# Half of the exponentials of some attention steps move from ScalarE to VectorE

## The chip, the core and the metric

The kernel runs on one core of a Trainium2 chip. The metric is the device time of one execution in microseconds (us). Four compute engines matter here: TensorE (PE in the profile; PEld is its loading of weights), VectorE (DVE), ScalarE (ACT) and GpSimd (POOL). Each works through its own instructions strictly in the order in which they were written, and waits for others by semaphores. TensorE writes its results into PSUM; ScalarE and VectorE read them there and write into SBUF.

## What is computed

The reference is a hybrid layer on an image batch of shape (4, 64, 64, 128), so 4 batches of 4096 tokens of 128 channels. All of it is float32.

1. Two 3x3 convolutions and a gate, then a first attention with one head (masked, 4 channels of keys, 16 of values) and a residual.
2. A second attention, over all 4096 tokens of a batch and not masked, with 16 heads of 8 channels:

```python
scores = jnp.einsum('bqhd,bkhd->bhqk', q, k)
probs = jax.nn.softmax(scores.astype(jnp.float32), axis=-1).astype(q.dtype)
attn = jnp.einsum('bhqk,bkhd->bqhd', probs, v).reshape(bsz, seqlen, DIM)
h = x + attn @ wo
ffn = jax.nn.silu(h @ w1) * (h @ w3) @ w2
```

3. Eight experts of 128x128 with the top two of a softmax router, and a residual.

The second attention is by far the largest part: 4 x 16 x 4096 x 4096, about 1.07 thousand million exponentials.

## The kernel before

**Steps.** The second attention is cut into *steps*. A step takes one batch, one group of four heads, one chunk of 512 queries (`c`) and one tile of 128 keys (`kt`); 4096 steps make up the whole. A step has two parts, made by `attention_step` (L774). `scores` lets TensorE multiply keys and queries with four matmuls into two PSUM tiles `s` of 128x1024 (two heads in each), and lets ScalarE turn each into an SBUF tile `e` of exponentials with one ACTIVATE. `values` lets TensorE multiply the exponentials with the values (and with a column of ones, for the sum of the softmax) and add the result up in the one PSUM tile `acc`. `acc` is started anew at the first key tile of a *segment* (most segments are 32 steps long) and copied out by VectorE into `at` at the last (L803 to L808).

**Buffers.** There are three `s` tiles (L134), eight `e` tiles (L130 and L144), one `acc` (L135) and, for all other products of TensorE, one tile `m` (L136). A tile that is asked for again waits until the last readers of its buffer are done.

**Order of the work.** Everything is unrolled in Python, and the class `InOrder` (L95) makes each engine keep the order in which instructions are written. A loop (L1184 to L1209) writes one *turn* after another. A turn does the following:

- `do_step` (L225): write the scores and exponentials of the next step and put it on the list `undone`;
- perhaps `insert` (L241): write one piece of other work, called *filler* here: a piece of a convolution, of the first attention, of a projection, of the feed-forward part or of the experts. A filler is a group of 4 to 16 matmuls into `m` and, often, VectorE instructions that read `m`. `credit` decides whether a turn has one: it grows by `rate` in every turn and is used up by the price that the filler yields (0.46 and 0.6 for the usual ones);
- `finish(2)` (L229): write the values of the oldest steps until only two are undone.

So in a steady stream TensorE's order in the turn of step k is: the scores of step k, a filler or nothing, the values of step k-2. The first attention's steps (`first_step`) pass through the same loop, two `e` tiles each as well. The first 330 us (the first batch's convolutions up to the first keys) and the last 70 us lie outside this stream.

The profile puts almost every instruction on one line, L105, since `InOrder` records them there. So groups are told apart by their tile names: `s<-qx,f_kx` is a score, `e<-s` an exponential, `acc<-e,vg` a value product, `m<-...` filler.

Of the kernel before, what the change touches and what calls it, by code (L numbers as in the profile page):

```python
# [9 lines left out]
FP = mybir.dt.float32  # L10
# [81 lines left out]
    return np.concatenate(list(parts.values()), axis=1), where  # L92


class InOrder:  # L95


    def __init__(self, tc, engine):
        self._tc, self._engine, self._last = tc, engine, None

    def __getattr__(self, name):
        op = getattr(self._engine, name)

        def call(*args, **kw):
            made = op(*args, **kw)  # L105
            if self._last is not None:
                after = mybir.DependencyInfo(mybir.DependencyClass.NoSync, mybir.DependencyReason.DATA)
                self._tc.add_manual_dep(made.ins, self._last, after, reason="as written")
            self._last = made.ins.name
            return made  # L110

        return call
# [3 lines left out]
def fast_path(ctx: ExitStack, tc: tile.TileContext, a: dict, where: dict, out: bass.AP, verdict):  # L116
# [10 lines left out]

    const = ctx.enter_context(tc.tile_pool(name="f_const", bufs=1))
    big = ctx.enter_context(tc.tile_pool(name="f_big", bufs=1))
    ep = ctx.enter_context(tc.tile_pool(name="f_ep", bufs=8))  # L130
    wk = ctx.enter_context(tc.tile_pool(name="f_wk", bufs=2))
    sm = ctx.enter_context(tc.tile_pool(name="f_sm", bufs=2))
    dram = ctx.enter_context(tc.tile_pool(name="f_dram", bufs=2, space=bass.MemoryType.DRAM))
# [15 lines left out]

    def chunk(tag, name=None):  # L150
        return wk.tile([P, QB], FP, tag=tag, bufs=CHUNKS.get(tag, 1), name=name or tag)

    def small(name, dims):
        return sm.tile([P, *dims], FP, tag=name, name=name)
# [64 lines left out]
    seen = const.tile([P, 4, B], FP, name="f_seen")  # L219


    steps_in, undone, fillers, urgent = [], [], [], []
    held, turn = [False], [0]

    def do_step(step):  # L225
        scores, values = step
        undone.append((values, scores()))

    def finish(leave):  # L229
        while len(undone) > leave:  # L230
            values, es = undone.pop(0)
            values(es)

    def advance(part):

# [463 lines left out]
    def first_step(c, r, qx0, sums, found):  # L699

        diagonal = r == c

        if diagonal and c > 0:
            place = [(0, 0, 0), (0, QB, P), (1, 2 * P, 2 * P), (1, QB, 3 * P)]
            spans = [(0, QB + 3 * P), (2 * P, QB + P)]
        else:
            place = [(j // 2, (j % 2) * QB, 0) for j in range(NSLOT)]
            spans = [(0, 2 * QB)] * 2

        def scores():  # L710
            ss, es = [s_tile(), s_tile()], [e_tile(), e_tile()]
            for j, (half, lo, off) in enumerate(place):
                r_ = slice(j * SLOT, j * SLOT + n_row)
                pe.matmul(
                    ss[half][:, lo : lo + QB - off],
                    lhsT=kx0[r_, r, :].bitcast(FR),
                    rhs=qx0[r_, off:].bitcast(FR),
                    start=True,
                    stop=True,
                )  # L720
            for e, s, (lo, hi) in zip(es, ss, spans):
                act.activation(e[:, lo:hi], s[:, lo:hi], AF.Exp)
            parts = []
            for j, (half, lo, off) in enumerate(place):
                e = es[half][:, lo : lo + QB - off]
                if diagonal:
                    at = j * P - off
                    if at:
                        pool.memset(e[:, :at], 0.0)
                    dve.tensor_tensor(e[:, at : at + P], e[:, at : at + P], k_of["tri"], ALU.mult)  # L730
                parts.append((off, e))
            return parts

        def values(parts):
            if r == 0:
                sums.append(acc if alone[0] else m_tile())
            for j, (off, e) in enumerate(parts):
                pe.matmul(
                    sums[0][j * SLOT : (j + 1) * SLOT, off:],
                    lhsT=v0[:, 4 * r + j, :],  # L740
                    rhs=e,
                    start=r == 0,
                    stop=r == c,
                )
            if r == c:
                at = chunk("at0")
                dve.tensor_copy(at, sums[0])
                found.append(at)

        return scores, values  # L750


    def keys(d, g, quarter, place):
# [17 lines left out]
        )  # L771
        return vg

    def attention_step(b, seg, kt, place, qx, vg, part):  # L774
        g, c = seg.g, seg.c

        def scores():
            ss, es = [s_tile(), s_tile()], []
            for j in range(NSLOT):
                r = slice(j * SLOT, (j + 1) * SLOT)  # L780
                pe.matmul(
                    ss[j // 2][:, (j % 2) * QB : (j % 2 + 1) * QB],
                    lhsT=kx[r, place * P : (place + 1) * P].bitcast(FR),
                    rhs=qx[r, :].bitcast(FR),
                    start=True,
                    stop=True,
                )
            for s in ss:
                e = e_tile()
                act.activation(e, s, AF.Exp)  # L790
                es.append(e)
            return es

        def values(es):
            for j in range(NSLOT):
                pe.matmul(
                    acc[j * SLOT : j * SLOT + 1 + HD1, :],
                    lhsT=vg[:, kt // 4, kt % 4, j, :],
                    rhs=es[j // 2][:, (j % 2) * QB : (j % 2 + 1) * QB],
                    start=kt == seg.lo,  # L800
                    stop=kt == seg.hi - 1,
                )
            if kt == seg.hi - 1:  # L803
                at = chunk("at1")
                if part:
                    dve.tensor_tensor(at, acc, part[0], ALU.add)
                else:
                    dve.tensor_copy(at, acc)  # L808
                if seg.hi == NT:
                    urgent.append((turn[0] + 1, lambda: by_token(b, g, c, at)))  # L810
                else:
                    sp.dma_start(out=scratch[b]["p"][g, c], in_=at)

        return scores, values

    def by_token(b, g, c, at):

# [300 lines left out]
    def stream():  # L1118
# [16 lines left out]
        for at, seg in enumerate(plan):  # L1135
            now[0] = seg.b
            while not seg.ready():
                yield None
            late = seg not in ahead
            if late:  # L1140
                bring(seg)
            qx, vg = ahead.pop(seg)
            part = []
            for quarter in range(seg.lo // 8, seg.hi // 8):
                key_quarter(seg, quarter)
            for _ in range(4 if late else 0):
                yield None
            follower = plan[at + 1] if at + 1 < len(plan) else None
            for kt in range(seg.lo, seg.hi):
                steps_left[seg.b] -= 1  # L1150
                if seg.lo > 0 and kt == seg.lo + 4:

                    part.append(chunk("part"))
                    sp.dma_start(out=part[0], in_=scratch[seg.b]["p"][seg.g, seg.c])
                yield attention_step(seg.b, seg, kt, 8 * seg.place(kt // 8) + kt % 8, qx, vg, part)
                if follower and follower not in ahead and follower.ready():
                    bring(follower)
                if kt % 8 == 7:

                    for later in plan[at + 1 :]:  # L1160
                        quarters = [q for q in range(later.lo // 8, later.hi // 8) if later.place(q) == seg.place(kt // 8)]
                        if quarters:
                            if later.ready():
                                key_quarter(later, quarters[0])
                            break
# [17 lines left out]
    credit, waiting = 0.0, False  # L1183
    while True:  # L1184
        turn[0] += 1
        if steps_in:
            do_step(steps_in.pop(0))
        else:
            step = next(steps, False)
            if step is False:  # L1190
                break
            waiting = step is None
            if waiting:
                finish(0)
            else:
                do_step(step)
        b = now[0]
        if batches[b].second == NQ and len(batches) == b + 1 and b + 1 < B:
            Batch(b + 1)
            fillers.append([first_attention(b + 1, batches[b + 1]), PREPARE])  # L1200

        rate = 1.0
        if batches[b].second == NQ:
            within = steps_left[b] - 40 if b + 1 < B else min(steps_left[b] - 40, 160)
            rate = sum(us for _, us in fillers) / max(1, within)
        credit = min(0.7, credit + rate)
        if waiting or credit > 0.0 or urgent and not held[0]:
            credit -= insert()
        finish(2)  # L1209
    finish(0)  # L1210
    while urgent:
        if held[0]:
# [722 lines left out]
```

## Time and profile before

| what | value |
|---|---|
| median of 3 runs | 8379.8 us (8378.74 to 8383.02) |
| profiled execution, its time | 8383.2 us |
| profiled execution, span from first to last instruction | 8381.4 us |
| mean granted TensorE clock | 0.981 |
| ACT busy | 7919.2 us (94%) |
| PE busy | 8082.3 us (96%) |
| DVE busy | 2543.8 us (30%) |
| POOL busy | 711.6 us (8%) |
| exponentials `e<-s` on ACT | 8480, 7836.1 us |
| value products `acc<-e,vg` on PE | 32768, 4362.5 us |
| scores `s<-qx,f_kx` on PE | 16960, 2795.9 us |

A group's row in the profile gives the engine, the operation, the output and inputs, the shape and the count, then after the bar the busy time in us and the mean duration of one in ns, then the idle time of the engine just before the group's instructions and what ended it. Matmuls overlap in time, so that a mean of 598 ns does not say that one takes 598 ns of TensorE; the distance from one start to the next is what counts. A float32 value product appears as two MATMUL records, a score as one; a group of four value products is therefore x8.

### The profile page before, as it was taken

What the parts mean: (1) busy time and instruction counts of PE and PEld (TensorE: products, weight loads), DVE (VectorE), ACT (ScalarE), POOL (GpSimd) and SP (SyncE); (2) the same over time, 40 slices, a digit from 0 to 9 for tenths busy, and PEclk for the clock granted to TensorE, in tenths of its full rate; (3) what the DMA queues carried; (4) which work ended last, traced back from release to release, by engine and by line L of the source; (5) the groups of instructions that cost most, each with busy time, mean ns of one, the idle gap of its engine ahead of it and who ended that gap; (6) DMA issues with size and microseconds to landing.
All of it is one profiled execution on the core that took longest, in us unless ns stands there. A gap on an engine that the chain in (4) does not pass through costs nothing. (4 is left out here: it accounts for less than half of the span.)

```text
span 8381.4 us, 173763 instructions
## 1 busy us (share of the span) xinstructions
PE 8082.3 (96%) x73785; PEld 2565.1 (31%) x73785; DVE 2543.8 (30%) x5279; ACT 7919.2 (94%) x8698; POOL 711.6 (8%) x597
## 2 busy tenths in 40 slices
PE   4899999999999999999999999999999999999998
PEld 3222222223333332333333233233333333332333
DVE  7433122223322223333332222333333332221123
ACT  1899999999999999999999999999999999999996
POOL 5101101000000003110000000311100000000000
PEclk7999999999999999999999999999999999999998
DMA  1221010101100001101110000001101111011110
GB/s 54 76 66 66 19 38 23 40 23 48 44 17 19 22 11 31 33 29 46 34 30 11 26 15 17 28 30 44 33 33 43 37 37 43 31 38 34 54 53 32
DMA packets 239541, 295.99 MB, mean 35 GB/s; under 512 B 81731, under 2 KB 153891, under 8 KB 238755
## 3 DMA queue, kind: packets, MB, share of 16 engines
q1 hardware_dynamic: 234739, 283.03, 10.6%
q8 instruction: 580, 9.50, 0.5%
q10 hardware_dynamic: 4016, 1.77, 0.1%
q14 instruction: 206, 1.69, 0.1%
HBM read 185.12 MB, written 99.61 MB: 34 GB/s over the span
## 5 line engine op out<-in xcount | busy, mean ns | idle before, releaser
L105 ACT ACTIVATE e<-s 128x1024 f32<-128x1024 f32 x8480 | 7836.1, 1083 | 191.0 <-PE s L105 180.7
L105 PE MATMUL acc<-e,vg 128*9 128x512 f32 x32768 | 4362.5, 598 | 61.2 <-DVE at L105 60.4
L105 PE MATMUL s<-qx,f_kx 32*128 32x512 f32 (+1 forms) x16960 | 2795.9, 497 | 68.3 <-ACT e L105 51.4
L105 PEld LDWEIGHTS s<-qx,f_kx 32*128 32x128 f32 (+1 forms) x16960 | 1121.4, 182 | 4074.7 <-ACT e L105 3821.9
L105 PEld LDWEIGHTS acc<-e,vg 128*9 128x9 f32 x32768 | 707.3, 90 | 861.3 <-issue 448.5
L105 PE MATMUL m<-v,f_wino 128*32 128x256 f32 x5360 | 435.1, 397 | 9.6 <-DVE t L105 7.1
L105 DVE TENSOR_TENSOR by_e<-m,gate 128x512 f32<-128x512 f32 x248 | 171.5, 691 | 869.3 <-PE m L105 869.3
L105 POOL TENSOR_TENSOR v<-r 128x1024 f32<-128x1024 f32 x128 | 249.4, 1954 | 1277.4 <-PE m L105 1258.1
L105 DVE COPY sd<-m 128x512 f32<-128x512 f32 x167 | 115.5, 691 | 726.0 <-PE m L105 726.0
L105 PE MATMUL m<-f_we,y2T 128*32 128x256 f32 x3968 | 318.4, 393 | 0.5 <-DVE nt L105 0.5
L105 POOL TENSOR_TENSOR rs<-ve,f_minus_half 128x4 f32<-128x4 f32 x64 | 65.2, 1019 | 2972.5 <-DVE ve L105 2819.6
L105 DVE TENSOR_REDUCE added<-by_e 128x128 f32<-128x1024 f32 x128 | 255.2, 1994 | 4.4
L105 POOL TENSOR_TENSOR t<-t,h 128x512 f32<-128x512 f32 x32 | 40.9, 1278 | 2456.3 <-DVE h L105 2456.3
L105 PE MATMUL m<-hT,f_fw 128*32 128x256 f32 (+1 forms) x2728 | 236.1, 391 | 0.0
L105 DVE TENSOR_TENSOR t<-m,sums 128x256 f32<-128x256 f32 x126 | 53.5, 425 | 465.5 <-PE m L105 465.5
L105 DVE SCALAR_TENSOR_TENSOR h<-m,h 128x512 f32<-128x512 f32 (+1 forms) x93 | 64.2, 690 | 411.3 <-PE m L105 411.3
L105 DVE TENSOR_TENSOR t<-m,t 128x512 f32<-128x512 f32 x62 | 42.9, 692 | 446.3 <-PE m L105 446.3
L105 DVE COPY h<-m 128x512 f32<-128x512 f32 (+1 forms) x93 | 64.2, 690 | 357.0 <-PE m L105 357.0
L105 PEld LDWEIGHTS m<-v,f_wino 128*32 128x32 f32 x5360 | 107.1, 108 | 177.2 <-issue 152.5
L105 DVE COPY at<-acc 128x512 f32<-128x512 f32 x130 | 89.6, 689 | 233.2 <-PE acc L105 232.7
L105 PE MATMUL m<-e,f_v 128*32 128x512 f32 (+2 forms) x1128 | 149.7, 574 | 0.0
L105 DVE TENSOR_TENSOR e<-e,f_consts 128x128 f32<-128x128 f32 x128 | 30.2, 295 | 346.9 <-ACT e L105 346.9
(259 smaller groups left out, 3751.3 us busy)
## 6 DMA issues: line engine op xcount, KB each, us to landing
f_kx<-d_k SPq DMA_DIRECT2D x139, 512.0 KB, 4.1
qx<-d_q SPq DMA_DIRECT2D x152, 256.0 KB, 2.7
d_q<-two SPq DMA_DIRECT2D x64, 512.0 KB, 3.6
vg<-d_v SPq DMA_DIRECT2D x32, 576.0 KB, 4.2
d_k<-two SPq DMA_DIRECT2D x32, 512.0 KB, 3.3
d_v<-vc SPq DMA_DIRECT2D x32, 288.0 KB, 3.1
xe<-in_x_dram SPq DMA_DIRECT2D x32, 256.0 KB, 2.9
xt<-in_x_dram SPq DMA_DIRECT2D x32, 256.0 KB, 3.8
```

The costliest lines, as they stand in the source:

```text
L105: made = op(*args, **kw)
```

## The change

In some steps, called *late* here (a name of the diff), only the first of the two `s` tiles is turned into exponentials by ScalarE. The second is read by VectorE, which computes the exponentials with a scaling, a rounding by adding a large constant, a polynomial of degree five in Horner form, and a shift that makes the power of two. These are 1 instruction of 1024 columns and 16 of 512 columns for each late step. They are not written at once: `settle` writes a few in each turn, as long as an estimate of VectorE's backlog (`dve.load`) is under 1.5 us. When all are written, and three turns have passed, `settle` writes the values of the late step, behind the ordinary values of that turn. At the end of a segment all that is left is written at once. There is at most one late step at a time, and it lies at least 2 steps behind the start of its segment and at least 8 ahead of its end.

The bookkeeping of `credit` follows: a late turn adds 0.92, the turn of the late values takes 0.97. A new tile set (`ea`, `z` of 1024 columns, `t`, `q` of 512 columns, one buffer each) holds the late step, and the pool of `e` tiles goes from eight buffers to five.

```diff
-    ep = ctx.enter_context(tc.tile_pool(name="f_ep", bufs=8))
+    ep = ctx.enter_context(tc.tile_pool(name="f_ep", bufs=5))
...
+    def late_tile(name, n=QB):
+        return ep.tile([P, n], FP, tag=name, bufs=1, name=name)
...
     def do_step(step):
-        scores, values = step
-        undone.append((values, scores()))
+        scores, values, late = step
+        es = scores()
+        if late is None:
+            undone.append((values, es))
+        else:
+
+            slow.append((values, es, late, turn[0]))
...
+    def settle(limit):
+
+        if not slow:
+            return 0.0
+        values, es, todo, since = slow[0]
+        if not todo and (limit is None or turn[0] > since + 2):
+            slow.pop(0)
+            values(es)
+            return 0.97
+        while todo and (limit is None or dve.load < limit):
+            todo.pop(0)()
+        if limit is None:
+            return settle(None)
+        return 0.0
+
+    def powers(z):
+
+        todo = []
+        for h in range(2):
+            zh = z[:, h * QB : (h + 1) * QB]
+            t, q = late_tile("t"), late_tile("q")
+            todo.append(lambda t=t, zh=zh: dve.tensor_scalar(t, zh, MAGIC, None, ALU.add))
+
+            todo.append(
+                lambda t=t, zh=zh: dve.scalar_tensor_tensor(zh, t, MAGIC, zh, ALU.subtract, ALU.subtract)
+            )
+            todo.append(lambda q=q, zh=zh: dve.scalar_tensor_tensor(q, zh, POLY[4], zh, ALU.add, ALU.mult))
+            for k in (3, 2, 1):
+                todo.append(
+                    lambda q=q, zh=zh, k=k: dve.scalar_tensor_tensor(q, q, POLY[k], zh, ALU.add, ALU.mult)
+                )
+            bits = t.bitcast(mybir.dt.int32)
+            todo.append(lambda bits=bits: dve.tensor_scalar(bits, bits, 23, None, ALU.logical_shift_left))
+            todo.append(
+                lambda t=t, q=q, zh=zh: dve.scalar_tensor_tensor(zh, q, POLY[0], t, ALU.add, ALU.mult)
+            )
+        return todo
...
+            if late is not None:
+                e, z = late_tile("ea", 1024), late_tile("z", 1024)
+                act.activation(e, ss[0], AF.Exp)
+                dve.tensor_scalar(z, ss[1], LOG2E, SHIFT, ALU.mult, ALU.add)
+                late.extend(powers(z))
+                return [e, z]
...
         def values(es):
+            if kt == seg.hi - 1:
+                settle(None)
...
-                yield attention_step(seg.b, seg, kt, 8 * seg.place(kt // 8) + kt % 8, qx, vg, part)
+
+                late = [] if not slow and seg.lo + 2 <= kt <= seg.hi - 8 else None
+                yield attention_step(seg.b, seg, kt, 8 * seg.place(kt // 8) + kt % 8, qx, vg, part, late)
...
     while True:
         turn[0] += 1
+        begun, spare = len(slow), 0.0
...
+        if len(slow) > begun:
+            spare = 0.92
+        dve.load = max(0.0, dve.load - 1.84 + spare)
...
-        credit = min(0.7, credit + rate)
+        credit = min(0.7, credit + rate) + spare
...
         finish(2)
+        credit -= settle(1.5)
```

`dve.load` grows in `InOrder` with each VectorE instruction by 0.15 + 0.00106 for each column.

More of the change, by code (lines that the diff above doesn't have):

```diff
@@ L92, in shape_constants @@
     return np.concatenate(list(parts.values()), axis=1), where
+LOG2E = 1.4426950408889634
+SHIFT = 0.4430875400888237
+POLY = (-753.21220293, 522.08671661, -180.9375242, 41.80864673, -7.28773528)
+MAGIC = 12582912.0 + 256 + 117
 class InOrder:
@@ L99, in __init__ @@
         self._tc, self._engine, self._last = tc, engine, None
+        self.load = 0.0
     def __getattr__(self, name):
@@ L105, in call @@
             made = op(*args, **kw)
+            sizes = [int(np.prod(ap.shape[1:])) for ap in (*args, *kw.values()) if hasattr(ap, "shape")]
+            self.load += 0.15 + 1.06e-3 * max(sizes, default=0)
             if self._last is not None:
@@ L219, in fast_path @@
     seen = const.tile([P, 4, B], FP, name="f_seen")
-    steps_in, undone, fillers, urgent = [], [], [], []
+    steps_in, undone, fillers, urgent, slow = [], [], [], [], []
     held, turn = [False], [0]
     def do_step(step):
-        scores, values = step
-        undone.append((values, scores()))
+        scores, values, late = step
[4 more added lines that the diff above has]
+            slow.append((values, es, late, turn[0]))
     def finish(leave):
@@ L748, in values @@
                 found.append(at)
-        return scores, values
+        return scores, values, None
     def keys(d, g, quarter, place):
@@ L772, in values_of, with attention_step @@
         return vg
-    def attention_step(b, seg, kt, place, qx, vg, part):
+    def attention_step(b, seg, kt, place, qx, vg, part, late):
         g, c = seg.g, seg.c
@@ L812, in values @@
                     sp.dma_start(out=scratch[b]["p"][g, c], in_=at)
-        return scores, values
+        return scores, values, late
     def by_token(b, g, c, at):
```

## The prediction

> **What bounds the kernel now.** I read the engine totals first, then the groups of instructions, then the engines by stretch, then the order of time in two single turns. Totals and groups:
>
> ```profile
> PE 8082.3 (96%) x73785; PEld 2565.1 (31%) x73785; DVE 2543.8 (30%) x5279; ACT 7919.2 (94%) x8698; POOL 711.6 (8%) x597
> ...
> L105 ACT ACTIVATE e<-s 128x1024 f32<-128x1024 f32 x8480 | 7836.1, 1083 | 191.0 <-PE s L105 180.7
> ```
>
> ScalarE makes 8480 exponentials and sits idle only 191.0 us ahead of them. TensorE's 96% says less, because its matmuls overlap. By stretch (columns: engine, busy us and count):
>
> ```profile
> 2330.00:3330.00 1000.00, 988.82 (x9034) 304.31 (x9032) 256.15 (x503) 990.55 (x1091) 72.75 (x55) 1.00 0.07 20
> ```
>
> The fourth pair is ACT: 990.55 of 1000 us. In the stream ScalarE is the bound, but with TensorE close behind. One turn with filler, and one without (start us, duration, engine, group):
>
> ```profile
> 4005.65 2.90 ACT L105 ACTIVATE e<-s 128x1024 f32<-128x1024 f32 x3
> 4005.91 0.50 PE L105 MATMUL s<-qx,f_kx 32*128 32x512 f32 x4
> 4006.34 0.64 PE L105 MATMUL m<-v,f_wino 128*32 128x256 f32 x8
> 4006.80 1.04 PE L105 MATMUL acc<-e,vg 128*9 128x512 f32 x8
> ```
>
> ```profile
> 4000.51 0.51 PE L105 MATMUL s<-qx,f_kx 32*128 32x512 f32 x4
> 4000.95 1.05 PE L105 MATMUL acc<-e,vg 128*9 128x512 f32 x8
> 4001.93 0.51 PE L105 MATMUL s<-qx,f_kx 32*128 32x512 f32 x2
> ```
>
> Three exponentials end 2.90 us after the first began and one lasts 1.08, so they start every 0.91 us: 4005.65, 4006.55, 4007.46. A turn has two, 1.81 us. On TensorE a turn without filler takes 1.42 us (4000.51 to 4001.93), one with filler 1.86 (the next scores start at 4007.77). Step k's scores start at 4005.91, its first exponential at 4006.55, its second at 4007.46: 1.55 us after the scores. In the same turn the values of step k-2 start at 4006.80 and end at 4007.84, 1.93 us after the scores. So in a filler turn **the second exponential of step k starts before the values of step k-2 are done**. Without filler the values end at 4002.00, 1.49 us after the scores. Keep these two numbers.
>
> **What the Trainium skill says.** "Perfetto Trace Analysis", section "Identifying Performance Opportunities": the same gap repeating on the engine that should be saturated can mean that there aren't enough buffers for the next tile. Before the change no such gap is seen (191 us in all). Its section "Identifying the Most-Contended Engine" warns that matmul busy time isn't distance to the limit; the trace agrees, since a turn of 1.81 us needs 1.42 without filler. "VectorE: DVE Perf Modes", section "The perf-mode tier table", has fp32 one-source operations within SBUF at twice the rate, and two-source ones or a PSUM operand at the single rate. The trace agrees: the cast `two<-u` takes 441 ns for 512 columns, the two-source `g0T<-th,h` 692, the copy `sd<-m` from PSUM 691.
>
> **The change, part by part.** The instruction order of the changed kernel, built but not run, holds 325 late steps.
>
> *Removed:* 325 exponentials x 0.91 = 296 us of ScalarE, 3.5%.
>
> *Added on VectorE:* per late step one 1024-column read of PSUM (nearest row, `top<-two` of 1024 columns: 1.22 us), 12 two-source instructions x 0.69 = 8.3 and 4 one-source ones x 0.49 (`w<-u`, 486 ns; between 0.44 and 0.64 by the rows) = 2.0: 11.5 us, x325 = 3740 us. VectorE goes from 2544 to about 6280 us, some 70% of its time: not the bound by sum.
>
> *Moved on TensorE:* no matmul is added. The late values come as a second group of 0.97 us in one turn (325 turns, 214 of them with filler too), and the late turn has no values at all.
>
> *The `e` pool, eight buffers to five.* This is where I expect the result to be decided. While step k's exponentials are written, steps k-2 and k-1 still hold two tiles each, as `finish(2)` leaves them; with step k that is six. With five, the second exponential of step k can only start when the first tile of step k-2 is free, that is when the values of step k-2 have been added up. These stand on TensorE behind step k's scores and behind the filler. In the built order the semaphores say so: 3,908 of the 3,915 ordinary second exponentials wait for the value matmuls of their own turn; before, all 4,240 wait for their scores alone.
>
> What the wait costs: the values end 1.93 us after the scores in a filler turn, and ScalarE needs about 0.10 more to see it (at 3083.4 a score ended at 3083.37 and ScalarE started at 3083.47): 2.03 us, against 1.55 before. So 0.48 us late. Without filler 1.49 + 0.10 = 1.59 against 1.55: nearly nothing. What is late next: the first exponential of step k+1, queued behind it, and with it the scores of step k+2, which need that exponential's PSUM tile (1.17 us from the start of a first exponential, 4004.74, to the scores at 4005.91). That closes a loop over two turns: 2.03 + 0.91 + 1.17 = 4.11 us with filler, where ScalarE alone needs 4 x 0.91 = 3.62. A filler turn that follows an undelayed one therefore takes 1.81 + 0.48; one right behind a delayed turn comes free, since the loop spans both. By this rule 1,294 ordinary turns of the built order are delayed (2,560 of 4,237 turns have filler): 1,294 x 0.48 = **621 us**.
>
> Nor does a late step then give its 0.91 back. The turn behind it has scores that wait for the late exponential, then values, then its own second exponential: the same loop, 3.67 us without filler and 4.11 with, for late turn and next. Two ordinary turns without the wait take 3.62. With filler in that next turn (240 of 325): 240 x 0.48 = **115 us**; the others 0. So the 296 us are not gained but swallowed.
>
> *Late values.* They put 0.97 us on TensorE behind the ordinary values, and the next scores wait. Without filler these start at 0.43 + 0.97 + 0.97 = 2.37 us, their exponential 0.60 later at 2.97, where ScalarE would be free at 1.55 + 0.91 = 2.46: 0.51 lost. With filler 3.43 against 2.03 + 0.91 = 2.94: 0.49, or up to 1.0 where an ordinary step follows. I take 0.52: 325 x 0.52 = **169 us**; both ends, 0.25 and 0.8, give 80 and 260.
>
> *Ends of segments.* By the rule of `settle`, 72 polynomial instructions are written at once at segment ends, ahead of the last values: 72 x 0.69 = **50 us**, or 0 if VectorE was ahead.
>
> *VectorE late for others.* `m` has one buffer. A filler's copy may find up to 1.5 + 0.69 us of polynomials ahead; after filler ends at 0.89 us the next `m` product comes at about 2.0 + 0.43, and the copy takes 0.76, so 0.78 is slack. `at<-acc` (154 of them) has less. Unknown: 0 to 150 us; I take **40**. One-source instructions may also meet GpSimd's; that is in the 150.
>
> *Taken back.* Other ACTIVATEs (some 180 in the stream x 0.65) fall half into ScalarE's new gaps: -60. Runs of filler turns that TensorE sets at 1.86 instead of 1.81 now vanish under the wait: about half of them, 1,300 x 0.05 = -65. TensorE's other small stalls: -30. `InOrder`'s count of columns writes no instruction; DMAs are unchanged in number.
>
> Sum: 621 + 115 + 169 + 50 + 40 - 155 = +840 us. On the profiled execution's span of 8381.4 that is 9221; the runs' median lies 1.6 us below that span, so I predict 9220 us.
>
> **Rivals.** (A) *The wait doesn't bind and the relief arrives.* For it: ScalarE is the bound, and 296 us less would show. Then late values still cost 169 and segment ends and lateness 90: 8381 - 296 + 259 = 8344, or 8085 if late values cost nothing and VectorE keeps ahead. It decides once the values end within 1.45 us of the scores in filler turns, where the rows have 1.93. Against it: the five buffers, and the order of TensorE.
> (B) *It binds half as hard*, because filler turns bunch up or the values' first half is done sooner: 368 in place of 736, giving 8840. Against it: the four products of a group run side by side (eight records of 598 ns within 1.04 us), so the first half ends with the second.
> (C) *VectorE becomes the second bound.* If a quarter of some 1,300 refills of `m` find it 0.7 us late beyond the slack, +230: 9440. For it: it is an in-order queue at 70%, and its polynomials stand behind copies that wait for TensorE. Against it: the estimate of the backlog, and longer turns leave it more time.
>
> **How the numbers follow.** Chances: main case 0.75, B 0.10, C 0.10, A 0.05. The main case's own bounds: 0.35 instead of 0.48 takes 200 off, cheap late values 90 more, and dear ones with a late VectorE add 240: about 8930 to 9450. B and C stretch it to 8840 and 9450, which I take as the range. A difference of 0.2% is about what a measurement of this kernel can tell from none. Faster: most of A, 0.04; same 0.01; slower 0.95.
>
> **What would show it.** Right: ACT well below 94% with a large idle time ahead of `e<-s`, ended by PE `acc`, some 0.3 us in many filler turns; 325 exponentials fewer; VectorE near 6200 us; TensorE's groups at the same durations. Wrong: idle time ahead of `e<-s` as small as now, or ended by `s` or by VectorE; or PE waiting for DVE `m` readers for hundreds of us. The prediction fails most easily if the second exponential's wait is released before the values end.

## The result and the profile after

The changed kernel takes 9103.9 us (median of 4 runs, 9095.4 to 9105.2); the kernel before took 8381.4 us in the same session (8378.7 to 8385.3). The ratio is 1.086, with a 95% interval of 1.0841 to 1.0878: slower by 722 us. The profiled execution has a span of 9102.9 us.

Engine totals of the changed kernel, and its group of ordinary exponentials (busy us, mean ns, then idle time ahead of the group and what ended it):

```profile
PE 8489.9 (93%) x73785; PEld 2743.8 (30%) x73785; DVE 6156.8 (68%) x10804; ACT 7823.0 (86%) x8373; POOL 756.0 (8%) x597
...
L116 ACT ACTIVATE e<-s 128x1024 f32<-128x1024 f32 x7830 | 7442.3, 1032 | 953.3 <-PE acc L116 838.5
```

ScalarE has 325 exponentials fewer in all (7830 `e` and 325 `ea` against 8480), as planned. But it is busy 86% instead of 94%, and idle 953.3 us ahead of exponentials instead of 191.0. Nearly all of it, 838.5 us, was ended by `acc`, a value product. In the kernel before no exponential waited for one. The waits of ScalarE (us in total, times, longest) say how often:

```profile
ACT e L116 <- PE acc L116: 838.5, 1498, 14.9
ACT e L116 <- PE s L116: 78.5, 100, 18.6
```

In the order of time one sees where (rows of PE and ACT alone). First the ends of two filler turns of the changed kernel, in a stretch of ordinary steps (start us, duration, engine, group, idle before):

```profile
4061.07 1.04 PE L116 MATMUL acc<-e,vg 128*9 128x512 f32 x8
4062.05 0.51 PE L116 MATMUL s<-qx,f_kx 32*128 32x512 f32 x4
4062.21 3.81 ACT L116 ACTIVATE e<-s 128x1024 f32<-128x1024 f32 x4 [0.21 <-PE acc L116]
...
4065.09 1.04 PE L116 MATMUL acc<-e,vg 128*9 128x512 f32 x8
4066.06 0.51 PE L116 MATMUL s<-qx,f_kx 32*128 32x512 f32 x4
4066.22 4.72 ACT L116 ACTIVATE e<-s 128x1024 f32<-128x1024 f32 x5 [0.20 <-PE acc L116]
```

The values end at 4062.11 and ScalarE restarts at 4062.21, 0.10 later; four exponentials on, two turns later, the same thing happens at 4066.22. Two filler turns take 4.01 us, where the prediction's loop gives 4.11 and two turns without the wait 3.62. Then the surroundings of a late step, whose first tile is `ea`:

```profile
4054.73 1.10 ACT L116 ACTIVATE ea<-s 128x1024 f32<-128x1024 f32 x1
4055.07 0.50 PE L116 MATMUL s<-qx,f_kx 32*128 32x512 f32 x2
4055.67 1.08 ACT L116 ACTIVATE e<-s 128x1024 f32<-128x1024 f32 x1
4055.89 0.49 PE L116 MATMUL s<-qx,f_kx 32*128 32x512 f32 x2 [0.32 <-ACT ea L116]
4056.47 0.66 PE L116 MATMUL m<-f_consts,at 128*128 128x128 f32 x4
4057.06 1.05 PE L116 MATMUL acc<-e,vg 128*9 128x512 f32 x8
4058.03 0.50 PE L116 MATMUL s<-qx,f_kx 32*128 32x512 f32 x4
4058.20 3.80 ACT L116 ACTIVATE e<-s 128x1024 f32<-128x1024 f32 x4 [1.45 <-PE acc L116]
```

ScalarE is done with the late step's one exponential early and then stands for 1.45 us, until the values that end at 4058.11 free its tile. The time that was taken off ScalarE comes back as its idle time. This holds for most late steps: counted in the trace, 295 of the 1,498 waits for values (347.3 of the 838.5 us) stand at just this place, the second exponential behind `ea`.

VectorE's new groups have about the durations that the prediction took for them (0.69 us for instructions with two sources, 0.49 for those with one, 1.22 for the read of PSUM); the column after the bar is busy us and mean ns:

```profile
L116 DVE SCALAR_TENSOR_TENSOR q<-q,z 128x512 f32<-128x512 f32 x1950 | 1408.4, 722 | 54.4
L116 DVE TENSOR_SCALAR z<-s 128x1024 f32<-128x1024 f32 x325 | 397.3, 1223 | 346.9 <-PE s L116 341.5
...
L116 DVE TENSOR_SCALAR t<-z 128x512 f32<-128x512 f32 x650 | 288.3, 444 | 14.5
```

### The profile page after: what moved, and what is told of

The parts are those of the page before. It is cut to its first block, busy times and chain, and to the rows that moved or that the text cites. A ratio compares the mean times of both kernels' runs of the same rounds, so it can differ in the third digit from the quotient of the medians.

```text
span 9102.9 us, 178435 instructions
## 1 busy us (share of the span) xinstructions
PE 8489.9 (93%) x73785; PEld 2743.8 (30%) x73785; DVE 6156.8 (68%) x10804; ACT 7823.0 (86%) x8373; POOL 756.0 (8%) x597
## 5 line engine op out<-in xcount | busy, mean ns | idle before, releaser
L116 ACT ACTIVATE e<-s 128x1024 f32<-128x1024 f32 x7830 | 7442.3, 1032 | 953.3 <-PE acc L116 838.5
L116 PE MATMUL s<-qx,f_kx 32*128 32x512 f32 (+1 forms) x16960 | 3142.2, 498 | 335.8 <-ACT e L116 179.3
L116 DVE SCALAR_TENSOR_TENSOR q<-q,z 128x512 f32<-128x512 f32 x1950 | 1408.4, 722 | 54.4
L116 DVE TENSOR_SCALAR z<-s 128x1024 f32<-128x1024 f32 x325 | 397.3, 1223 | 346.9 <-PE s L116 341.5
L116 DVE SCALAR_TENSOR_TENSOR z<-q,t 128x512 f32<-128x512 f32 x650 | 471.3, 725 | 17.6
L116 DVE SCALAR_TENSOR_TENSOR z<-t,z 128x512 f32<-128x512 f32 x650 | 470.5, 724 | 17.4
L116 DVE SCALAR_TENSOR_TENSOR q<-z 128x512 f32<-128x512 f32 x650 | 465.7, 717 | 18.3
L116 PE MATMUL acc<-z,vg 128*9 128x512 f32 x1300 | 375.4, 599 | 51.4 <-DVE z L116 51.4
L116 ACT ACTIVATE ea<-s 128x1024 f32<-128x1024 f32 x325 | 336.0, 1034 | 44.4 <-PE s L116 41.3
L116 PE MATMUL acc<-ea,vg 128*9 128x512 f32 x1300 | 335.0, 593 | 0.0
```

## The experiments

The theory: five `e` tiles make the second exponential of a step wait for values that stand behind the filler, this makes the loss, and it swallows the relief of late steps as well. The rivals: the pool is innocent and late steps cost the time, by VectorE's in-order queue or by their values. All medians below are of four runs or more; each ratio is against runs of the kernel before on the same chip.

### The pool alone

```diff
-    ep = ctx.enter_context(tc.tile_pool(name="f_ep", bufs=8))
+    ep = ctx.enter_context(tc.tile_pool(name="f_ep", bufs=5))
```

This is the kernel before with that one line, or with six tiles instead.

> The kernel before with one edit: five e buffers instead of eight; no late steps, all exponentials on ScalarE. Theory (the buffer wait makes the loss): in the built order 1,520 filler turns follow an undelayed one, 1,520 x 0.48 = 730 us, less the 155 taken back as in the prediction: about 8955 us (8800 to 9120), ACT idle ahead of e<-s some 700 us, ended by PE acc. Rival (VectorE's polynomials and the late values make the loss, the pool is innocent): 8380 us.

> The kernel before with six e buffers instead of eight. Theory: two unfinished steps and the present one hold six tiles, so six make no step wait: 8380 us, within 0.3%. Rival (any cut of the pool costs, since ScalarE needs to run ahead): about 8550 us.

Measured: five tiles 8894.6 us, ratio 1.0606 (1.0589 to 1.0624); six tiles 8380.3 us, ratio 0.9999 (0.9990 to 1.0008). The group of exponentials, first with five tiles, then with six:

```profile
L105 ACT ACTIVATE e<-s 128x1024 f32<-128x1024 f32 x8424 | 7958.1, 1036 | 559.7 <-PE acc L105 486.8 <-PE s L105 45.6 <-PE m L105 9.0
```

```profile
L105 ACT ACTIVATE e<-s 128x1024 f32<-128x1024 f32 x8424 | 7805.9, 1084 | 192.9 <-PE s L105 184.5 <-ACT e L105 0.4
```

So one line makes 513 of the 722 us. From eight tiles to six nothing is lost; the step from six to five costs everything. The idle time of 486.8 us came in 1,499 waits of 0.32 us each. That is less than the delay, since two exponentials back to back overlap in the records (here 1.04 us long and 0.92 from start to start), and a late one has lost this overlap as well. From the start of the exponential before to the start of one that waited for values the trace has 1.37 us on average, 0.45 more than 0.92; by the median it is 1.28, or 0.36 more. Forecast were 0.48 us a time and 1,520 turns.

### The same five tiles, values ahead of the filler

```diff
-        if waiting or credit > 0.0 or urgent and not held[0]:
-            credit -= insert()
         finish(2)
+        if waiting or credit > 0.0 or urgent and not held[0]:
+            credit -= insert()
```

Once in the kernel before with five tiles, once in the changed kernel.

> Five e buffers as in pool5_alone, but each turn writes the values of the step before last ahead of the filler, so that they end about 1.49 us after the scores in every turn. The same instructions in number and kind. Theory: the wait is still in the program but ends at 1.59 us instead of 2.03, against 1.55 needed: 8380 to 8480 us. Rival (five buffers cost wherever the filler stands): about 8955 us, as pool5_alone.

> The changed kernel, five buffers, with the same swap: values of the step before last ahead of the filler. 319 late steps. Theory: the wait no longer binds, the relief of 319 x 0.91 = 290 us arrives, less late values (319 x 0.52 = 166) and 90 for segment ends and lateness: about 8350 us (8230 to 8450). Rival (late values and VectorE's in-order queue make most of the loss): 8850 us or more.

Measured: 8435.1 us, ratio 1.0061 (1.0044 to 1.0078), for the first. The same five tiles and the same wait in the program cost 53 us instead of 513 when no filler stands ahead of the values. ScalarE waits for values 59 times in this kernel, with the longest wait last in the row, and not 1,499 times:

```profile
ACT e L105 <- PE acc L105: 60.5, 59, 4.4
```

That settles the first half of the theory: with five tiles it is the place of the values on TensorE, behind the filler, that makes the wait. (This order with eight tiles was not run, so how much of the 53 us is due to the order itself is open.)

The second missed clearly: 8852.8 us, ratio 1.0557 (1.0539 to 1.0575), where I had expected 8350. Late steps make the kernel 418 us slower than `pool5_values_first`, so the relief did not arrive. The wait is not gone here either. It has left most ordinary turns, but not the late steps:

```profile
ACT e L116 <- PE acc L116: 319.2, 367, 13.6
```

Counted in the trace, 265 of these 367 waits (176.9 us) stand at the second exponential behind `ea`. One of them (rows of PE and ACT alone):

```profile
3040.84 1.04 ACT L116 ACTIVATE ea<-s 128x1024 f32<-128x1024 f32 x1
3041.74 1.06 ACT L116 ACTIVATE e<-s 128x1024 f32<-128x1024 f32 x1
3041.93 0.49 PE L116 MATMUL s<-qx,f_kx 32*128 32x512 f32 x2 [0.34 <-ACT ea L116]
3042.36 1.05 PE L116 MATMUL acc<-e,vg 128*9 128x512 f32 x8
3043.33 0.66 PE L116 MATMUL m<-f_consts,at 128*128 128x128 f32 x4
3043.50 2.05 ACT L116 ACTIVATE e<-s 128x1024 f32<-128x1024 f32 x2 [0.70 <-PE acc L116]
```

No filler stands ahead of the values, and still they end only at 3043.41, since the scores before them had to wait for `ea`'s PSUM tile. ScalarE could have gone on at 3042.65 (3041.74 + 0.91) and starts at 3043.50, 0.85 us later: nearly the whole 0.91 of the late step. The prediction's own rule said so (3.67 us for a late turn and the next without filler, against 3.62); the expectation for this run overlooked it. What remains to be found is what polynomials and late values add.

### Late steps without their polynomials, and without their values

```diff
-                late.extend(powers(z))
+                late.extend([count] * 16)
```

Here `count` only advances `dve.load`, so that all else stays in its place. The other edit drops `values(es)` of the late step in `settle`. Each was made in the changed kernel and in `changed_values_first`.

> The changed kernel without the 16 polynomial instructions of each late step: z is only scaled, so its values are not exponentials; the estimate of VectorE's load is advanced as if they were there, so that late steps, fillers and late values stand where they stood. 325 late steps, VectorE 3,400 us less busy. As predicted (polynomials cost 50 at segment ends and 40 by lateness): about 9015 us (8950 to 9070). Theory 2 (VectorE's in-order queue makes most of what late steps cost beyond the pool, since readers of m and acc stand behind polynomials): 8900 us or less, that is 200 or more below the changed kernel.

> The changed kernel without the four value products of each late step (their part of the sum is left out); the polynomials stay, and credit is charged as before. As predicted (0.52 us for each second group of values): 9104 - 169 = 8935 us (8840 to 9020). Theory 2 (VectorE's queue makes the rest): little changes but the waits for z at late values, some 130 us by the profile's DVE z rows: about 8900 to 9000, so this run alone does not tell them apart; with changed_no_polynomial it does.

> changed_values_first (8853 us) without the polynomial instructions, z only scaled, VectorE's load estimate advanced as if they were there; 318 late steps. As predicted (90 us for segment ends and lateness): about 8760 us. Theory 2 (VectorE's queue turns the relief into a loss): 8500 us or less. If late values are what costs (theory 3: 1.2 us and more for each, not 0.52): 8700 us or more.

> changed_values_first (8853 us) without the value products of late steps (left out of the sum); polynomials stay. As predicted (0.52 us each): about 8690 us. Theory 2 (VectorE's queue): 8600 us or more, since its copies of m and acc are as late as before. Theory 3 (late values cost 1.2 us and more each): 8450 us or less.

| late steps with | changed kernel's order | values first |
|---|---|---|
| polynomials and values | 9103.9 | 8852.8 |
| values, no polynomials | 8962.5 | 8585.4 |
| polynomials, no values | 8995.9 | 8590.2 |
| no late steps, five tiles | 8894.6 | 8435.1 |

In the changed kernel polynomials are worth 141 us and late values 108. Both results there lie within what the prediction's terms gave (8950 to 9070, and 8840 to 9020). In the other order each is worth more, 267 and 263, and both kernels are faster than those terms gave, by 175 and 100 us (8760 and 8690). A likely reason, not tested by itself, is that ScalarE waits for values less often there (367 times against 1,498), so that less of TensorE's delay falls into time in which ScalarE stands anyway. Together the two are more than the 418, and neither theory 2 nor theory 3 as written holds alone: both overlap in one wait. The waits of TensorE for `z` in `changed_values_first`, and then in `first_no_polynomial` (weight loads PEld and matmuls PE wait over the same time, so the two rows are not to be added):

```profile
PEld acc L116 <- DVE z L116: 164.7, 126, 10.2
PE acc L116 <- DVE z L116: 85.3, 43, 9.2
```

```profile
PEld acc L116 <- DVE z L116: 1.7, 7, 0.2
```

Late values wait for a polynomial that is not finished; take away either and that wait is gone. The waits behind `ea` stay in both of these kernels (266 and 258 of them, 181.6 and 191.4 us), so most of the relief is missing there too. By an estimate from the row above, 265 x 0.85 = 225 of some 290 us are swallowed; the other 65 and the 418 make 483 us of cost, and the two parts, at most 530 together and less by what they share, can account for it.

### The relief alone

Now both edits together: late steps hand their second tile to VectorE, which scales it, and nothing else follows. Without the polynomials' `t` and `q` there is room for a sixth `e` tile.

```diff
-                late.extend(powers(z))
+                late.extend([count] * 16)
...
             slow.pop(0)
-            values(es)
             return 0.97
...
-    ep = ctx.enter_context(tc.tile_pool(name="f_ep", bufs=5))
+    ep = ctx.enter_context(tc.tile_pool(name="f_ep", bufs=6))
```

The last edit is in the six-tile kernel only; `six_late_values` keeps `values(es)`.

> The changed kernel with only the relief left: late steps give their second tile to VectorE, which only scales it; no polynomial and no late values (both left out of the result); five e buffers; late steps and fillers stand where they stood. 325 late steps. Theory (the two-turn loop over the fifth buffer swallows the 296 us): as pool5_alone, 8895 us (8840 to 8930). Rival (the relief arrives, and polynomials and late values eat it up): 8600 us.

> As five_relief_only, with six e buffers, for which there is room once the polynomial's two tiles are gone. Theory: no wait on values, the relief arrives: 8380 - 296 = 8085 us (8060 to 8200; the upper end if TensorE's turns of 1.86 us begin to bind). Rival (the relief is lost in any case, since a late turn's scores and filler keep TensorE as long as ScalarE was kept): 8380 us.

> As six_relief_only, but with the late steps' value products (of scaled scores, not of exponentials). Theory of the prediction (0.52 us each where ScalarE sets the pace): six_relief_only + 169. Rival (a second group of values costs its whole 0.97 us, or more with the filler beside it): six_relief_only + 315 or more, so that the relief is gone.

Measured: with five tiles 8897.5 us, ratio 1.0617 (1.0599 to 1.0635). That is `pool5_alone`'s 8894.6 to within its scatter: 296 us of exponentials taken off ScalarE gain nothing. With six tiles 8336.4 us, ratio 0.9949 (0.9932 to 0.9965): a gain of 48 us, not of 296. So here my theory fell. The rival's 8380 us was much nearer. No exponential waits for values any more in this kernel, and five sixths of the relief are lost all the same. ScalarE's idle time ahead of exponentials in `six_relief_only`:

```profile
L116 ACT ACTIVATE e<-s 128x1024 f32<-128x1024 f32 x7774 | 7280.0, 1064 | 375.8 <-PE s L116 365.0 <-ACT e L116 1.9
```

It now waits for scores, 365.0 us against 184.5 with six tiles and no late steps. The order of time around one late step of that kernel (rows of PE and ACT alone):

```profile
3184.97 1.03 ACT L116 ACTIVATE ea<-s 128x1024 f32<-128x1024 f32 x1
3185.14 0.50 PE L116 MATMUL s<-qx,f_kx 32*128 32x512 f32 x2 [0.23 <-ACT e L116]
3185.87 1.96 ACT L116 ACTIVATE e<-s 128x1024 f32<-128x1024 f32 x2
3186.05 0.49 PE L116 MATMUL s<-qx,f_kx 32*128 32x512 f32 x2 [0.41 <-ACT ea L116]
3186.47 0.64 PE L116 MATMUL m<-v,f_wino 128*32 128x256 f32 x8
3186.93 1.04 PE L116 MATMUL acc<-e,vg 128*9 128x512 f32 x8
3187.90 0.51 PE L116 MATMUL s<-qx,f_kx 32*128 32x512 f32 x4
3188.34 0.64 PE L116 MATMUL m<-v,f_wino 128*32 128x256 f32 x8
3188.50 1.94 ACT L116 ACTIVATE e<-s 128x1024 f32<-128x1024 f32 x2 [0.67 <-PE s L116]
```

The late step k gives ScalarE back at 3185.87, 0.90 us after it took it, and step k+1's first exponential starts at once. But step k+1's second pair of scores needs the PSUM tile that `ea` reads, and starts at 3186.05, when `ea` has ended. Behind it on TensorE stand the filler and the values, 1.85 us, and only then the scores of step k+2. ScalarE runs dry at 3187.83 and restarts at 3188.50. The two turns take 0.90 + 2.63 = 3.53 us instead of 3.62 to 3.72. Counted in the trace, 288 of ScalarE's 434 waits for scores (233.1 of 366.8 us) stand at just this place, the third exponential behind `ea`.

By the same arithmetic, from the first exponential of the late step: the next scores' second half starts at about 1.08 to 1.17, TensorE's turn adds 1.42 without filler or 1.86 with, the exponential follows 0.60 later, at about 3.2 or 3.6; ScalarE alone would be there at 2.72. So a filler in the next turn (240 of 325) loses the whole 0.91 and none loses about half: 85 x 0.45 = 38 us of gain, beside 48 measured. The trace bears this out: the third exponential behind `ea` starts 3.74 us after it where the next turn has a filler (median of 217 late steps with none but ordinary exponentials behind them), and 3.19 us where it has none (65); four ordinary exponentials in `pool6_alone` take 3.67. TensorE is not full by sum: by the turns of the built order 2,560 x 1.86 + 1,677 x 1.42 = 7143 us, an estimate, of some 7930 in the stream. That three `s` tiles and this order on TensorE are the cause is read from the trace and these sums; a kernel with a fourth `s` tile was not tried. There is no room for one: by the Trainium skill ("Trainium Kernel Development and Optimization", section "NeuronCore Architecture") PSUM has 2 MiB in 128 partitions, that is 4096 float32 columns, and three `s` tiles, `acc` and `m` take 3 x 1024 + 512 + 512 = 4096; no run here went beyond that.

`six_late_values`: 8515.7 us, ratio 1.0165 (1.0148 to 1.0182), which is 179 us above `six_relief_only`, or 0.55 us for each of 325 second groups of values (forecast 0.52).

### A whole version with six tiles

```diff
-    ep = ctx.enter_context(tc.tile_pool(name="f_ep", bufs=5))
+    ep = ctx.enter_context(tc.tile_pool(name="f_ep", bufs=6))
...
-            t, q = late_tile("t"), late_tile("q")
+            t, q = late_tile("t"), chunk("part", "q")
...
-                late = [] if not slow and seg.lo + 2 <= kt <= seg.hi - 8 else None
+                late = [] if seg.b > 0 and not slow and seg.lo + 2 <= kt <= seg.hi - 8 else None
...
-        if waiting or credit > 0.0 or urgent and not held[0]:
+        heavy = bool(slow) and not slow[0][2] and turn[0] > slow[0][3] + 2
+        if waiting or not heavy and (credit > 0.0 or urgent and not held[0]):
             credit -= insert()
         finish(2)
-        credit -= settle(1.5)
+        credit -= settle(0.75)
```

and `at1` with one buffer instead of two, for the room.

> A whole version: six e buffers (q shares the tile of part and late steps are left to batches 1 to 3; at1 has one buffer), no filler in the turn of late values, and polynomials written only while the estimated backlog is under 0.75 us instead of 1.5. 189 late steps. Theory: relief 172 us less late values 0.51 x 189 = 96 and polynomials (0.84 us a late step by the runs so far, halved by the smaller backlog) 80: about 8385 us, between 8310 and 8440. Rival (the smaller backlog makes polynomials free): 8310 us or less.

Measured: 8555.0 us, ratio 1.0203 (1.0186 to 1.0220), above the range. The expectation still let the whole relief arrive (172 us). With the 48 of 325 that `six_relief_only` showed, 189 late steps bring about 28; late values at 0.51 and polynomials at the 80 assumed would make 8385 - 28 + 96 + 80 = 8533, so that by this estimate most of the miss is the relief. What the single buffer of `at1` and the shared tile of `q` cost by themselves was not measured. Its polynomials are not free: TensorE's weight loads wait 77.4 us for `z` ahead of late values. No version found here beats the kernel before by making exponentials on VectorE.

## Why the prediction was right

9220 us were forecast, with 8840 to 9450 as range; 9103.9 were measured. By its steps:

- **The `e` pool.** The deciding step held. Forecast for five tiles: 621 + 115 - 155 = 581 us with late steps in place; measured 513 without them (`pool5_alone`, 8894.6 - 8381.9) and 513 with the relief (`five_relief_only`, 8897.5 - 8384.7). ScalarE waited 1,498 times for values, where the rule gave 1,294 ordinary and 240 late-pair delays, 1,534. The size of one delay was somewhat too large: forecast 0.48, in `pool5_alone` 0.45 on average and 0.36 by the median, in the two filler turns above 4.01 - 3.62 = 0.39. With the average, 1,499 x 0.45 = 675 us, of which 162 do not show in the 513; what is taken back (155) has no measurement of its own, so how the 68 us too many divide between the two terms is open.
- **Swallowed relief.** Right: 3 us between `pool5_alone` and `five_relief_only`, and with five tiles also in its reason, since the waits behind `ea` end with values (295 of 325 late steps in the changed kernel). What the prediction did not see is that the `e` tiles are not the only reason: the three `s` tiles and TensorE's order take five sixths of the relief without them (`six_relief_only`).
- **Late values.** Forecast 169 us; 65 us without polynomials (8962.5 - 8897.5), 108 when taken out of the whole kernel. Mis-sized for five tiles. Where the `e` wait is absent, the 0.52 us each are met: 179 us in `six_late_values`. So the wait hides part of them; how, was not traced.
- **Polynomials** (50 at segment ends, 40 for lateness): 98 us without late values (8995.9 - 8897.5), 141 out of the whole. Too small a term, and partly for another reason than the two named: late values wait for `z` (82.2 us of TensorE's weight loads in 43 waits in the changed kernel, its matmuls 51.4 us within the same time), which the prediction did not list.
- The late-step costs together: forecast 169 + 90 = 259, measured 9103.9 - 8897.5 = 206. The errors offset each other in part, which is luck.
- **VectorE by sum**: 6157 us, 68%, against 6280 and 70%.
- **Rival A** was wrong at its root, not only in its condition: even with no wait for values most of the relief does not come (`six_relief_only`), and with late values on top, still without polynomials, the kernel takes 8515.7 us. Its 8344 us was reached by no version that computes all exponentials.
- **Rival B** (half as hard) is refuted by `pool5_alone`. **Rival C** overstated VectorE: all polynomials together are worth 141 us, where it put 230 on top of 90, and TensorE's waits for readers of `m` stayed at tens of us each.
- **Small sums.** B's 368 instead of 736 makes 8852 us and not 8840, C's 230 makes 9450 and not 9440, and the dear ends of late values and lateness add 91 + 110 = 201 and not 240. None of them decides anything.

## What to carry to other kernels

Count the tiles that unfinished steps hold before cutting a pool: with two steps left undone and one begun, two tiles each, six tiles cost nothing here and five cost 6%, because the reader that frees the tile stands in another engine's queue behind unrelated filler. Taking work off the saturated engine gains only if the next work reaches it sooner: follow the freed time through the buffers (here PSUM score tiles) and the in-order queue that refills them, before adding up what was removed.

## What the runs showed of the hardware that was not expected

The records of exponentials got shorter where ScalarE waits more: 1084 ns on average before, 1036 with five tiles and 1034 in the changed kernel, for the same instruction, while consecutive starts lie about 0.91 us apart (0.92 with five tiles). So an idle time in the profile understates a delay by the overlap of two exponentials, and ScalarE's busy time went up with five tiles (8075.9 us against 7919.2 before, same instructions) while it did nothing more: busy time counts overlapping records once, and gaps remove overlap.

A few of VectorE's polynomial instructions took up to 2.3 us, where the median of the same group is 0.69. The row gives shortest, median and longest in ns:

```profile
L116 DVE SCALAR_TENSOR_TENSOR q<-q,z x1950: 668/692/2311, 461.0 to 9017.1; 128x512 f32<-128x512 f32 x195
```

The trace shows what goes with it. Of the changed kernel's 5,200 polynomial instructions, of one source and of two, 163 took over a quarter longer than the median of their group, 160 us more in all. Each of these 163 overlaps an instruction of GpSimd, which is busy 8% of the time; of the other 5,037 only 59 do. A run without GpSimd's work was not made, so the cause is not shown.
